# Products on column tiles, an FFN in 11 chunks and other orders of sums in a latent-attention kernel with an FFN gate

## The chip, the cores and the metric

The kernel runs on one core of one Trainium2 chip. The time is device microseconds of one execution; runs are compared by their median. Engines: TensorE (PE in the profile; PEld are its weight loads), VectorE (DVE), ScalarE (ACT), GpSimd (POOL), and SyncE (SP), which only issues transfers here.

## The reference

The input x has 8 sequences of 256 tokens with 512 features, all in fp32. What is computed, cut to what matters:

```python
xn = layernorm(x)                                  # over the 512 features
c_q, c_kv = xn @ Wq_down, xn @ Wkv_down            # 512 -> 64 each
q_c = (c_q @ Wq_up)    # 128 heads of 4            k_c, v_c = c_kv @ Wk_up, c_kv @ Wv_up
q_r = xn @ Wq_rope     # 128 heads of 64           k_r = xn @ Wk_rope   # 64, shared by the heads
scores = (q_c . k_c + q_r . k_r) / sqrt(68)        # per sequence and head, 256 x 256
s = softmax(scores) @ v_c  ->  @ Wo                # 512 -> 512
lin(x, wq, A, B) = x @ tile(wq, 4).T + 0.5 * x @ A.T @ B.T     # FFN, hidden 1376, rank 2
g = silu(lin2(silu(lin1(xn)) * lin3(xn)))
out = x + s * g
```

The FFN's weights repeat four times along their input. So x @ tile(wq, 4).T is the sum of the four quarters of x, 128 features wide, times wq.

## The kernel before, in words

All queues are filled in the order of the program text; no scheduler moves anything. Each engine runs its instructions in that order, and all transfers stand in one queue on SP. PSUM is a pool of eight banks of 128 x 512 (`bank`).

**First phase (`first_phase`, L286).** It runs over four blocks of 512 tokens. `norm` (L337) normalizes four tiles of x on DVE, `turn` (L364) transposes them on TensorE (xpt, L370) and adds the quarters (xsum). `narrow` (L392) and `down` (L402) make the products over xn (pm, pp, L387) and keep them in DRAM; `down` also calls `sum_x` (L141), which writes three quarters of xn to DRAM as they are and makes four differences on POOL (L154) for the later products. Then come six units u of two pairs: `low` (L410) writes the rank-2 products of four row-tiled matmuls into four banks (px and py, L420), `main` (L425) adds the 128-wide products onto them (L434, L435), ACT takes silu of px (L437) and DVE multiplies with py (L438) into hT. The hidden 1376 is four quarters of 344, each cut in chunks of 128, 128 and 88; hence 12 chunks for each of the two products. After units 2, 4 and at the end of the block `low_out` (L440) makes the rank-2 product mid2 on column tiles of 32 (its bank is pm, L449) and sums hT over the four quarters on POOL (L460 to L462, the result is h). `gate_out` (L472) then makes four products pf over three chunks each (L477), ACT takes silu into gs (two buffers), and gs goes to DRAM (L482). In the last block the steps of `between` (L554) put the first work of attention among the units: load and sum weights (`sum_w`, L126), `prepare` (qk, L240), `values` (vps, column tiles of 32, L267) and four `Project`s.

**Project (L177).** The query product with Wq_rope is made with a scheme of seven 256-column products in place of eight. Each product is two matmuls of 128 x 128 weights (`product`, L165; the matmul is L168, its banks are named q), so a Project has 14. ACT copies four banks (L208), POOL and DVE combine them (L213 to L226).

**Attention.** 64 steps n (sequence and group of 16 heads), each in two halves. A half has 48 score matmuls, four side by side on 32 rows (L618), eight maxima on DVE (L631), 16 exponentials on ACT (L637), eight transposes on DVE (L647), and one Project for a step two ahead, until all 128 are made. The first half also has `weigh` (av, L664, four side by side on 32 columns, for the step before) and, for some n, `prepare` and `values`. `normalize` (L692) divides by the sums. `put` (L723) multiplies with Wo (po, L727), `give` (L735) multiplies by the gate on DVE, adds x on POOL and stores; `finish` is both. Six of eight sequences are finished within the loop, at the end of second halves. The last two are written out at the end of the text:

```python
    weigh(last, 0)
    gather(last, early)
    for b in (B - 2, B - 1):
        for i in range(2):
            put(b, i, range(KT - 1))
    weigh(last, 1)
    gather(last, late)
```

then the two normalizations, the last chunk of every po and the four `give`s.

Of the kernel before, what the change touches and what calls it, by code (L numbers as in the profile page):

```python
# [15 lines left out]
P = 128  # L16
# [8 lines left out]
NTB = NT // TB  # L25
F = 1376
FQ = F // 4
CH = [(0, 128), (128, 128), (256, 88)]
EPS = 1e-5
QSCALE = float((HD + R) ** -0.5)  # L30

# [2 lines left out]
def mla_ffn_gate_kernel(  # L34
# [122 lines left out]
    def load_xs(p):  # L157

        if p < B // 2:
            xsums[p] = {}  # L160
            for i in (0, 4, 5, 3, 1, 6, 2):
                xsums[p][i] = xsp.tile([P, 2, S], F32, tag=f"x{i}", name=f"x{i}_{p}")
                nc.sync.dma_start(out=xsums[p][i], in_=xs_d[p][:, i])

    def product(bank_, w, x, first):  # L165

        for c in range(2):
            nc.tensor.matmul(  # L168
                bank_,
                w[:, c],  # L170
                x[:, c],
                start=first and c == 0,
                stop=c == 1,
                skip_group_check=True,
            )

    class Project:  # L177

# [57 lines left out]
    def prepare(b, g):  # L236


        qk = bank(f"qk_{b}_{g}")
        nc.tensor.matmul(qk[:, :S], wupq_sb[:, g, :], acts[b][:, 0, :], start=True, stop=True)  # L240
        nc.tensor.matmul(qk[:, S:], wupk_sb[:, g, :], acts[b][:, 0, :], start=True, stop=True)  # L241
        qc = qcp.tile([P, S], F32, tag="qc", name=f"qc_{b}_{g}", bufs=3)
        nc.scalar.copy(qc, qk[:, :S])  # L243
        kc = qcp.tile([P, S], F32, tag="kc", name=f"kc_{b}_{g}", bufs=3)
        nc.scalar.mul(kc, qk[:, S:], QSCALE)
        qks[b, g] = qc, kc
# [39 lines left out]
    def first_phase(between):  # L286
# [3 lines left out]

        ck_sb = fw.tile([P, KT, P], F32, name="ck_sb")
        cks_sb = fw.tile([P, 1], F32, name="cks_sb")
        w1_sb = fw.tile([P, F], F32, name="w1_sb")
        w3_sb = fw.tile([P, F], F32, name="w3_sb")
        b13_sb = fw.tile([98, F], F32, name="b13_sb")
        w2_sb = fw.tile([P, 3, D], F32, name="w2_sb")
        a2_sb = fw.tile([P, 4, 3, 32], F32, name="a2_sb")
        f1 = pool("f1", 1, st)
# [3 lines left out]
        def load_x(tb):  # L302
            xts[tb] = []
            for n in range(4):
                t = f1.tile([P, D], F32, tag="xt", name=f"xt_{tb}_{n}", bufs=6)
                nc.sync.dma_start(out=t, in_=x[ds(tb * TB + n * P, P), :])
                xts[tb].append(t)

        load_x(0)
        with tc.tile_pool(name="ckr", bufs=1) as ckr:  # L310
            kr_raw = ckr.tile([P, KT, R], F32, name="kr_raw")
# [14 lines left out]
        nc.sync.dma_start(out=wdn_sb, in_=w_down.rearrange("(c p) m -> p c m", p=P))  # L326
        for n in range(2):
            for k in range(2):
                nc.sync.dma_start(
                    out=b13_sb[64 * n + 32 * k : 64 * n + 32 * k + 2, :],  # L330
                    in_=b13[32 * k : 32 * k + 2, :],
                )
        nc.sync.dma_start(out=w1_sb, in_=w1t)
        nc.sync.dma_start(out=w3_sb, in_=w3t)
        load_x(1)

        def norm(tb):  # L337
# [46 lines left out]
        def over_xn(tb, name, weights):  # L384
            ps = bank(f"{name}_{tb}")
            for c in range(KT):
                nc.tensor.matmul(  # L387
                    ps, weights[:, c, :], xnT[tb][:, c, :], start=(c == 0), stop=(c == KT - 1)
                )
            return ps  # L390

        def narrow(tb):  # L392
# [9 lines left out]
        def down(tb):  # L402
            c = f1.tile([P, TB], F32, tag="tmp", name=f"c_{tb}")
            nc.scalar.copy(c, over_xn(tb, "pp", wdn_sb))
            nc.sync.dma_start(out=cs_d[tb], in_=c)
            sum_x(tb, xnT[tb])

        sets, hTs, h4s, mid2ps = {}, {}, {}, {}

        def low(tb, u):  # L410

            n, qp = divmod(u, 2)
            off, rows = CH[n]
            sets[tb, u] = []
            for i in range(2):
                cols = ds((2 * qp + i) * FQ + off, rows)
                for k in range(2):
                    ps = bank(f"p{'xy'[k]}_{tb}_{u}_{i}")
                    r = slice(64 * i + 32 * k, 64 * i + 32 * k + 2)
                    nc.tensor.matmul(  # L420
                        ps[:rows, :], b13_sb[r, cols], mids[tb][r, :], start=True, stop=False
                    )
                    sets[tb, u].append(ps)

        def main(tb, u):  # L425
            n, qp = divmod(u, 2)
            off, rows = CH[n]
            if qp == 0:
                hTs[tb, n] = f2.tile([P, 4, TB], F32, tag="hT", name=f"hT_{tb}_{n}")
            for i in range(2):  # L430
                q = 2 * qp + i
                cols = ds(q * FQ + off, rows)
                px, py = sets[tb, u][2 * i : 2 * i + 2]
                nc.tensor.matmul(px[:rows, :], w1_sb[:, cols], xsum[tb], start=False, stop=True)  # L434
                nc.tensor.matmul(py[:rows, :], w3_sb[:, cols], xsum[tb], start=False, stop=True)  # L435
                gate = f2.tile([P, TB], F32, tag="gate", name=f"gate_{tb}_{u}_{i}")
                nc.scalar.activation(gate[:rows, :], px[:rows, :], AF.Silu)  # L437
                nc.vector.tensor_mul(hTs[tb, n][:rows, q, :], gate[:rows, :], py[:rows, :])  # L438

        def low_out(tb, n):  # L440


            off, rows = CH[n]
            h = hTs.pop((tb, n))
            if n == 0:
                mid2ps[tb] = bank(f"pm2_{tb}")
                h4s[tb] = f1.tile([P, 3, TB], F32, tag="h4", name=f"h4_{tb}")
            for q in range(4):
                nc.tensor.matmul(  # L449
                    mid2ps[tb][32 * q : 32 * q + 32, :],  # L450
                    a2_sb[:rows, q, n, :],
                    h[:rows, q, :],
                    start=(n == 0),
                    stop=(n == 2),
                )
            if n == 2:
                nc.gpsimd.memset(h4s[tb][64:96, n, :], 0.0)
            h4 = h4s[tb][:rows, n, :]
            h4b = f1.tile([P, TB], F32, tag="h4b", name=f"h4b_{tb}_{n}")
            nc.gpsimd.tensor_add(h4, h[:rows, 0, :], h[:rows, 1, :])  # L460
            nc.gpsimd.tensor_add(h4b[:rows], h[:rows, 2, :], h[:rows, 3, :])
            nc.gpsimd.tensor_add(h4, h4, h4b[:rows])  # L462
            if n == 2:
                m2 = mid2ps.pop(tb)
                to = h4s[tb][96:128, n, :]
                nc.scalar.mul(to, m2[0:32], 0.5)
                for q in range(1, 4):
                    nc.vector.scalar_tensor_tensor(
                        to, m2[32 * q : 32 * q + 32], 0.5, to, ALU.mult, ALU.add
                    )  # L470

        def gate_out(tb):  # L472
            for n in range(4):
                tt = ds(n * P, P)
                pf = bank(f"pf_{tb}_{n}")
                for k in range(3):
                    nc.tensor.matmul(  # L477
                        pf, h4s[tb][:, k, tt], w2_sb[:, k, :], start=(k == 0), stop=(k == 2)
                    )
                gs = f2.tile([P, D], F32, tag="gs", name=f"gs_{tb}_{n}")  # L480
                nc.scalar.activation(gs, pf, AF.Silu)
                nc.sync.dma_start(out=gates_d[4 * tb + n], in_=gs)  # L482

        norm(0)
        turn(0)
        narrow(0)
# [4 lines left out]
        for tb in range(NTB):  # L491
            more = tb + 1 < NTB
            for u in range(6):
                low(tb, u)
                main(tb, u)
                if u in (2, 4):
                    low_out(tb, u // 2 - 1)
                if u == 1 and more:
                    norm(tb + 1)
                if u == 1 and tb + 2 < NTB:  # L500
                    load_x(tb + 2)
                if tb == NTB - 2 and u == 1:
                    between(1)
                if not more:
                    between(u + 2)
            if more:
# [4 lines left out]
            else:  # L511
                low_out(tb, 2)
            gate_out(tb)
        between(8)
        st.close()

# [206 lines left out]
    def put(b, n, chunks):  # L723
        if (b, n) not in pos:
            pos[b, n] = bank(f"po_{b}_{n}")
        for c in chunks:
            nc.tensor.matmul(  # L727
                pos[b, n],
                outT[b][:, c, ds(n * P, P)],
                wo_sb[:, c, :],  # L730
                start=(c == 0),
                stop=(c == KT - 1),
            )

    def give(b, n):  # L735
        g, xr = gxs.pop((b, n))
        nc.vector.tensor_mul(g, pos[b, n], g)  # L737
        nc.gpsimd.tensor_add(g, g, xr)
        nc.sync.dma_start(out=out[ds(b * S + n * P, P), :], in_=g)

    def finish(b, n):
# [10 lines left out]
    for n, (b, sg) in enumerate(blocks):  # L752
        for half in range(2):
# [18 lines left out]
            else:  # L772
                for r in range(4):
                    exponentials(n, two, r)
            for r in range(4):
                transpose(n, one, r)
            for r in range(2):
# [15 lines left out]
            if half == 0:  # L793
# [13 lines left out]
                        values(b + 1)  # L807
                if sg == 2 and b >= 2:
                    load_act(b + 2)
            elif n in outs:  # L810
                finish(*outs[n])


    early, late = ds(0, P), ds(P, P)
    weigh(last, 0)
    gather(last, early)
    for b in (B - 2, B - 1):
        for i in range(2):
            put(b, i, range(KT - 1))
    weigh(last, 1)  # L820
    gather(last, late)
    load_out(B - 2, 0)
# [2 lines left out]
    load_out(B - 1, 1, True)  # L825
    normalize(last - 1)
    normalize(last, early)
    put(B - 2, 0, [KT - 1])
    put(B - 2, 1, [KT - 1])
    put(B - 1, 0, [KT - 1])  # L830
    give(B - 2, 0)
    give(B - 2, 1)
    normalize(last, late)
    put(B - 1, 1, [KT - 1])
    give(B - 1, 0)
    give(B - 1, 1)


# [64 lines left out]
```

## Time and profile before

| | |
|---|---|
| three runs | 2059.2, 2064.73, 2066.32 us; median 2064.73 |
| the profiled execution | 2066.51 us, its span 2064.7 us |
| first phase, until the first scores start | 258.0 us |
| last scores of the loop end | 2039.7 us |
| maxima (L631) and transposes (L647) on DVE | 635.7 and 635.1 us busy |
| exponentials on ACT (L637) | 817.1 us busy |
| transfers | 183.15 MB, mean 89 GB/s |

How to read the profile: the page gives the busy time of each engine and the chain of work that ended last, followed back from the last instruction to what released each step. The same chain can be listed in order of time, merged where one line follows itself: start, length, engine, tile, line, count. The view by windows gives for a stretch its length, the busy time of an engine with the number of instructions, the granted TensorE clock, the share and the rate of DMA. An x before a number is a count. A matmul of fp32 operands is written once and stands in the trace as two records. Idle time of an engine is put down to what ended it.

### The profile page before, as it was taken

Reading aid. Unit: us, or ns where it says so; the run is one execution under the profiler, and the core shown is the slowest. Engines: PE = TensorE matmul, PEld = TensorE weight load, DVE = VectorE, ACT = ScalarE, POOL = GpSimd, SP = SyncE. Lnnn points to the kernel's source line nnn. Section 1 sums busy time; section 2 is a strip of 40 time slices with the busy share of each in tenths; the row PEclk is TensorE's granted clock in tenths of the full one; section 3 lists DMA queues with packets and bytes.
Section 4 is the critical chain, followed back from the end, with each engine's and each line's share of the span. In section 5 each row is a group of like instructions: output and inputs, shape, how many; then the busy total and the mean of one; then the engine's idle time right before and its main releaser. Section 6 shows DMA issues by size and latency. Waiting matters only on the chain.

```text
span 2064.7 us, 61156 instructions
## 1 busy us (share of the span) xinstructions
PE 2037.4 (99%) x25536; PEld 1665.3 (81%) x25536; DVE 1526.4 (74%) x2605; ACT 1084.0 (52%) x2991; POOL 718.4 (35%) x1039
## 2 busy tenths in 40 slices
PE   7999999999999999999999999999999999999998
PEld 3334588888888888888888888888888888888885
DVE  5332177878888777878788777878786867888788
ACT  2222265555655645465556554555555545555654
POOL 5334535544453232323332233223323223232232
PEclk9999999999999999999999999999999999999999
DMA  4233232222223132312223123222222222222212
GB/s 164 84 110 120 77 114 83 83 72 75 83 83 129 63 109 83 112 64 84 83 83 116 66 90 115 81 83 83 69 95 101 85 91 78 83 83 76 70 53 68
DMA packets 115447, 183.15 MB, mean 89 GB/s; under 512 B 8730, under 2 KB 81050, under 8 KB 115172
## 3 DMA queue, kind: packets, MB, share of 16 engines
q1 hardware_dynamic: 115172, 179.23, 25.2%
q8 instruction: 203, 3.33, 0.6%
q14 instruction: 72, 0.59, 0.1%
HBM read 145.12 MB, written 34.08 MB: 87 GB/s over the span
## 4 chain that ended last, share of the span: by engine, by line
PE 97%; DVE 1%; POOL 1%; DMA 0%; issue 0%; ACT 0%; POOLq 0%; SPq 0%; ACTq 0%; DVEq 0%
PE q L168 39%; PE sc L618 33%; PE av L664 11%; PE po L727 2%; PE px L434 2%; PE pf L477 2%; PE py L435 2%; PE px L420 1%; PE pm L387 1%; PE vps L267 1%; PE qk L240 1%; PE qk L241 1%; PE pp L387 1%; PE pm L449 1%; PE xpt L370 0%; DVE pt L647 0%
## 5 line engine op out<-in xcount | busy, mean ns | idle before, releaser
L637 ACT ACTIVATE pr<-sc,nmx 128x256 f32<-128x256 f32 x2048 | 817.1, 503 | 487.5 <-DVE nmx L631 486.0
L631 DVE TENSOR_REDUCE nmx<-sc 128x2 f32<-128x512 f32 x1024 | 635.7, 683 | 343.4 <-PE sc L618 314.2
L647 DVE STREAM_TRANSPOSE pt<-pr 128x512 f32<-128x512 f32 x1024 | 635.1, 678 | 0.0
L618 PE MATMUL sc<-act,qr 32*128 32x256 f32 x8192 | 492.1, 374 | 0.7 <-issue 0.6
L168 PE MATMUL q<-x,ws 128*128 128x256 f32 x2048 | 483.9, 379 | 0.0
L213 POOL TENSOR_TENSOR e<-e,e 128x256 f32<-128x256 f32 x128 | 93.1, 727 | 1083.6 <-ACT e L208 558.7
L618 PEld LDWEIGHTS sc<-act,qr 32*128 32x128 f32 x8192 | 423.5, 185 | 23.2 <-issue 1.4
L168 PEld LDWEIGHTS q<-x,ws 128*128 128x128 f32 x2048 | 389.0, 190 | 51.4 <-issue 0.2
L168 PE MATMUL q<-x,w 128*128 128x256 f32 x1536 | 387.4, 388 | 1.0 <-ACT pr L637 1.0
L168 PEld LDWEIGHTS q<-x,w 128*128 128x128 f32 x1536 | 291.5, 196 | 70.6 <-ACT pr L637 40.9
L618 PE MATMUL sc<-kc,qcm 32*128 32x256 f32 x4096 | 284.0, 387 | 2.1 <-DVE g L737 1.5
L618 PEld LDWEIGHTS sc<-kc,qcm 32*128 32x128 f32 x4096 | 199.8, 184 | 51.5 <-issue 24.2
L664 PEld LDWEIGHTS av<-pt,vpad 128*32 128x32 f32 x8192 | 219.6, 110 | 22.0 <-POOL e L214 8.0
L664 PE MATMUL av<-pt,vpad 128*32 128x128 f32 x8192 | 237.1, 273 | 0.0
L208 ACT COPY e<-q 128x256 f32<-128x256 f32 x512 | 203.6, 399 | 16.6 <-PE q L168 16.4
L684 ACT ACTIVATE acc<-av,sides_sb 128x256 f32<-128x256 f32 (+1 forms) x130 | 54.2, 468 | 235.7 <-PE av L664 235.7
L252 POOL TENSOR_TENSOR qcm<-qc,mask_sb 128x1024 f32<-128x1024 f32 x64 | 122.3, 1911 | 6.5 <-ACT qc L243 6.5
L438 DVE TENSOR_TENSOR hT<-gate,py 128x512 f32<-128x512 f32 (+1 forms) x48 | 32.5, 685 | 109.1 <-PE py L435 108.9
L215 POOL TENSOR_TENSOR qr<-e,e 128x256 f32<-128x256 f32 x128 | 93.6, 731 | 10.0
L214 POOL TENSOR_TENSOR e<-e,e 128x256 f32<-128x256 f32 x128 | 93.3, 729 | 10.0
L282 POOL COPY vpad<-vall 32x128 f32<-32x128 f32 x256 | 76.4, 298 | 18.9 <-ACT vall L274 5.8
L225 DVE TENSOR_TENSOR qr<-e,q 128x256 f32<-128x256 f32 x128 | 54.0, 422 | 29.1 <-PE q L168 20.6
(92 smaller groups left out, 1124.9 us busy)
## 6 DMA issues: line engine op xcount, KB each, us to landing
w<-in_w_rope_dram SPq DMA_DIRECT2D x128, 512.0 KB
ws<-sums_d SPq DMA_DIRECT2D x96, 512.0 KB
sums_d<-ws SPq DMA_DIRECT2D x32, 512.0 KB
x<-xs_d SPq DMA_DIRECT2D x28, 256.0 KB
xt<-in_x_dram SPq DMA_DIRECT2D x16, 256.0 KB
xs_d<-xt SPq DMA_DIRECT2D x16, 256.0 KB
gate_d<-gs SPq DMA_DIRECT2D x16, 256.0 KB
g<-gate_d SPq DMA_DIRECT2D x16, 256.0 KB
```

Source lines behind the costliest of these rows:

```text
L168: nc.tensor.matmul(bank_, w[:, c], x[:, c], start=first and c == 0, stop=c == 1, skip_group_check=True,)
L208: nc.scalar.copy(self.e[i], self.banks[i])
L213: nc.gpsimd.tensor_add(m6, m6, m1)
L214: nc.gpsimd.tensor_add(m7, m7, m6)
L215: nc.gpsimd.tensor_add(self.out(1, 1), self.split(m7), self.split(m5))
L252: nc.gpsimd.tensor_mul(qcm, qks[b, sg // 2][0].rearrange("p (q i) -> p q i", i=32).unsqueeze(2).to_broadcast([P, 8, 4, 32]), mask_sb[:, ds ...
L282: nc.gpsimd.tensor_copy(vpad[rows, :, :, 8 * t + 4 * (sg % 2) :][..., :4], valls[b][rows, :, sg])
L618: nc.tensor.matmul(sc[r][:, h, :], lhs.rearrange("p t i -> p (t i)"), rhs, start=(part == 0 and h == 0), stop=(part == 2), skip_group_chec ...
L631: nc.vector.tensor_reduce(nmx[:, r, :], scs[n, f][r], AX.X, ALU.max, negate=True)
L637: nc.scalar.activation(p[:, h, :], scs[n, f][r][:, h, :], AF.Exp, bias=nmxs[n, f][:, r, h : h + 1])
L647: nc.vector.transpose(pts[n, f // 2, r].rearrange("p k q i -> p q k i")[:, ds(2 * (f % 2), 2)], prs.pop((n, f, r)).rearrange("p h (k j) -> ...
L664: nc.tensor.matmul(av[32 * r : 32 * r + 32, ds(half * P, P)], vpad[:, k, r, :], pt[r][:, k].rearrange("p q i -> p (q i)"), start=(k == 0), ...
```

## The change

- A helper `on_columns` replaces one matmul of 128-wide weights by four with 32 columns of the weights each, which write to 32 partitions of the same bank each. It is used for all products that had 128-wide weights in `product`, `prepare`, `over_xn`, `main`, `gate_out` and `put`. Scores, the low products and the transposes stay as they are.
- The FFN's chunks of 88 in four quarters become three chunks of 128: the first 96 rows of chunk 8 + m hold the 88 of quarter m and zeros, the last 32 rows hold a third of the fourth quarter. The weights are loaded in pieces to match, four transfers in place of one for each of six pieces, and POOL sets zeros first. For these chunks the product on DVE is two instructions. The last unit has one chunk.
- The sums of hT on POOL are a function of their own, `fold`, called ahead of `low_out`, and for the last chunk right after unit 5, ahead of the `between` step there.
- `sum_x` leaves `down` and comes after unit 2 of the block (in the last block after unit 0).
- `gate_out` takes four banks at once and makes the first two chunks of all four products before the third chunk of any.
- 16 transposes of the identity come before the first `norm`.
- An exponential of one column comes on ACT behind the last `gate_out`.
- In step 62 `finish` comes ahead of the transposes of its half. At the end, the first three chunks of po are made ahead of the last `weigh` for one sequence, not two; the rest follows it in another order, and the last addition is on DVE.

```diff
+    def on_columns(to, w, x, start, stop):
+        for t in range(4):
+            tile_ = slice(32 * t, 32 * t + 32)
+            nc.tensor.matmul(to[tile_], w[:, tile_], x, start=start, stop=stop, skip_group_check=True)
+
     def product(bank_, w, x, first):
         for c in range(2):
-            nc.tensor.matmul(bank_, w[:, c], x[:, c], start=first and c == 0, stop=c == 1, ...)
+            on_columns(bank_, w[:, c], x[:, c], first and c == 0, c == 1)
...
+        def load_chunks(to, of):
+            of = of.rearrange("p (q f) -> p q f", q=4)
+            nc.sync.dma_start(
+                out=to[:, 0:8].rearrange("p (q n) m -> p q (n m)", q=4), in_=of[:, :, 0:256]
+            )
+            nc.sync.dma_start(out=to[:, 8:11, 0:88], in_=of[:, 0:3, 256:344])
+            nc.sync.dma_start(
+                out=to[:, 8:10, 96:128],
+                in_=of[:, 3, 256:320].rearrange("p (m i) -> p m i", m=2),
+            )
+            nc.sync.dma_start(out=to[:, 10, 96:120], in_=of[:, 3, 320:344])
+
+        for t in (w1_sb, w3_sb, b13_sb):
+            nc.gpsimd.memset(t[:, 8:11, 88:96], 0.0)
+            nc.gpsimd.memset(t[:, 10, 120:128], 0.0)
...
             nc.sync.dma_start(out=cs_d[tb], in_=c)
-            sum_x(tb, xnT[tb])
...
+        def pair(u):
+            return [2 * (i % 4) + i // 4 if i < 8 else i for i in range(2 * u, min(2 * u + 2, NCH))]
...
-                nc.tensor.matmul(px[:rows, :], w1_sb[:, cols], xsum[tb], start=False, stop=True)
-                nc.tensor.matmul(py[:rows, :], w3_sb[:, cols], xsum[tb], start=False, stop=True)
+                on_columns(px, w1_sb[:, c], xsum[tb], False, True)
+                on_columns(py, w3_sb[:, c], xsum[tb], False, True)
                 gate = f2.tile([P, TB], F32, tag="gate", name=f"gate_{tb}_{u}_{i}")
-                nc.scalar.activation(gate[:rows, :], px[:rows, :], AF.Silu)
-                nc.vector.tensor_mul(hTs[tb, n][:rows, q, :], gate[:rows, :], py[:rows, :])
+                nc.scalar.activation(gate, px, AF.Silu)
+                if c < 8:
+                    nc.vector.tensor_mul(h[:, c // 2, :], gate, py)
+                else:
+                    m = c - 8
+                    nc.vector.tensor_mul(h[0:96, m, :], gate[0:96], py[0:96])
+                    nc.vector.tensor_mul(
+                        h[32 * m : 32 * m + 32, 3, :], gate[96:128], py[96:128]
+                    )
...
         def gate_out(tb):
+            pfs = [bank(f"pf_{tb}_{n}") for n in range(4)]
+            for ks in ((0, 1), (2,)):
+                for n in range(4):
+                    for k in ks:
+                        on_columns(
+                            pfs[n], h4s[tb][:, k, ds(n * P, P)], w2_sb[:, k, :], k == 0, k == 2
+                        )
...
+        idle = bank("idle")
+        for n in range(16):
+            nc.tensor.transpose(idle[:, ds(n % 4 * P, P)], ident, ident)
         norm(0)
...
                 if u in (2, 4):
+                    fold(tb, u // 2 - 1)
                     low_out(tb, u // 2 - 1)
                 if u == 1 and more:
                     norm(tb + 1)
+                if u == (2 if more else 0):
+                    sum_x(tb, xnT[tb])
...
+                if u == 5:
+                    fold(tb, 2)
                 if not more:
                     between(u + 2)
...
             gate_out(tb)
+        nc.scalar.activation(cks_sb, cks_sb, AF.Exp)
         between(8)
...
-    def give(b, n):
+    def give(b, n, engine=nc.gpsimd):
         g, xr = gxs.pop((b, n))
         nc.vector.tensor_mul(g, pos[b, n], g)
-        nc.gpsimd.tensor_add(g, g, xr)
+        engine.tensor_add(g, g, xr)
...
+            if n == last - 1 and half:
+                finish(*outs[n])
             for r in range(4):
                 transpose(n, one, r)
...
     weigh(last, 0)
     gather(last, early)
-    for b in (B - 2, B - 1):
-        for i in range(2):
-            put(b, i, range(KT - 1))
+    for i in range(2):
+        put(B - 2, i, range(KT - 1))
     weigh(last, 1)
...
     normalize(last, early)
-    put(B - 2, 0, [KT - 1])
-    put(B - 2, 1, [KT - 1])
+    normalize(last, late)
+    put(B - 1, 0, range(KT - 1))
+    for i in range(2):
+        put(B - 2, i, [KT - 1])
     put(B - 1, 0, [KT - 1])
-    give(B - 2, 0)
-    give(B - 2, 1)
-    normalize(last, late)
-    put(B - 1, 1, [KT - 1])
-    give(B - 1, 0)
-    give(B - 1, 1)
+    put(B - 1, 1, range(KT))
+    for b in (B - 2, B - 1):
+        for i in range(2):
+            give(b, i, nc.vector if (b, i) == (B - 1, 1) else nc.gpsimd)
```

## The prediction

> **What bounds the kernel now.** I read the page first (busy shares, then the chain that ended last), next the chain in order of time in three stretches, and last the granted clock around the places where TensorE stood still. The page:
>
> ```profile
> PE 2037.4 (99%) x25536; PEld 1665.3 (81%) x25536; DVE 1526.4 (74%) x2605; ACT 1084.0 (52%) x2991; POOL 718.4 (35%) x1039
> ...
> PE q L168 39%; PE sc L618 33%; PE av L664 11%; PE po L727 2%; PE px L434 2%; PE pf L477 2%; PE py L435 2%; PE px L420 1%; PE pm L387 1%; PE vps L267 1%; PE qk L240 1%; PE qk L241 1%; PE pp L387 1%; PE pm L449 1%; PE xpt L370 0%; DVE pt L647 0%
> ```
>
> TensorE carries 97% of the chain, so every nanosecond it gives back counts until another engine is late. A product written once shows as two records here (28 for the 14 of a Project); I call one such record, or four side by side in tiles, a pass. The chain in order of time (start, length, what), from the attention loop:
>
> ```profile
> 474.39 5.39 PE sc L618 x96
> 479.78 6.25 PE q L168 x28
> 486.03 3.63 PE av L664 x128
> 489.66 5.39 PE sc L618 x96
> ...
> 706.53 3.63 PE av L664 x128
> 710.16 1.75 PE vps L267 x64
> ```
>
> and from the first phase:
>
> ```profile
> 210.25 1.06 PE px L434 x2
> 211.31 0.86 PE py L435 x2
> ...
> 213.88 6.04 PE q L168 x28
> ```
>
> The same 28 passes take 6.25 after the scores and 6.04 after py, which is also an untiled product. 6.04 / 28 = 215.7 ns is therefore the pass itself, and 0.21 the price of entering untiled products from row tiles. px says the same: 1.06 after the row-tiled low products against 0.86 in the middle, 0.20. vps runs on column tiles of 32 and follows av on such tiles: 1.75 / 16 = 109.2 ns a pass and no entry price. av after q is 3.63 - 32 x 0.1092 = 0.136. At 2039.70 av follows scores, not q, and 64 records take 1.89 = 1.75 + 0.14. So there are three prices: 0.21 into 128-wide weights from another layout, 0.136 into 32-wide ones, 0 within one layout. Scores pay 0.21 after q as after av (5.39 both times).
>
> **Column tiles, steady part.** q becomes 3584 passes of four instructions. Both ends: 32-wide passes of 128 columns take 109.2, twice that is 218.4, +2.7 ns a pass or +9.7 us; pm2 (32-wide, 512 columns, 0.99 for two) takes (0.99 - 0.136) / 2 = 427 ns against 429 for the untiled py, -1 ns at 256 columns or -3.6 us. I take 0: 256 columns lie between the two, and so does 0. A rule speaks against this change. The Trainium skill, "TensorEngine Tiling (Array Packing)", section Instruction Overhead, gives each matmul some 60 cycles; at the 2.4 GHz of "TensorE: Matmul & The Clock Gate" that is 25 ns. Added for three more instructions a pass, an estimate from these pages, it is 3584 x 75 ns = 269 us. The av row has 8192 records in 64 x 3.63 us, 28 ns each with their work in it, so the overhead lies under the neighbours' streaming; four in 215.7 ns are more thinly spread still. I follow the row.
>
> **Column tiles, entries.** Scores to q, 124 times (128 Projects, four of them in the first phase): 0.21 to 0.136, -9.1 (ends: 0, if the mode and not the width sets the price, and -9.1). q or qk to av, 61 times: 0.136 to 0, -8.3 (ends 0 and -8.3; av to vps is the same transition). In the first phase: low to px 24 x 0.065 = -1.6; px/py to pm2, to vps, and the last Project to pm2: 10 x 0.136 = -1.4; after pm2 the next product is in its layout: 3 x 0.20 + 2 x 0.21 + 0.20 = -1.2. The transposes stay untiled, so px/py to xpt newly pays 3 x 0.20, xpt to pm in block 0 0.14: +0.7. Together -20.9. What is late next: DVE waited for scores 126 times, 314.2 us in all, 2.5 each; a half loses under 0.25, so DVE stays ahead. If it did not, this part would stop there.
>
> **FFN in 11 chunks.** Each block's last unit keeps one chunk of two, so four of its eight px and py passes go, 4 x 0.429 = 1.72 us; the low products run side by side on row tiles and save nothing. Four blocks make 6.9, less 0.2 since 88-wide entries (1.02 for 1.06) become 128 wide: -6.7. DVE gets two more products of 0.68 a block; it idles 1 us between such products, and if that cover were gone it would be 1.4 a block.
>
> **fold and gate_out.** The last block ends like this:
>
> ```profile
> 242.32 0.74 POOL qr L215
> 243.11 0.53 POOL h L457
> ...
> 246.28 1.26 POOL h L462
> 247.53 0.04 issue
> 247.58 10.53 PE pf L477 x20
> 258.11 0.03 ACTq L481
> 258.14 0.04 issue
> 258.18 0.60 ACT gs L481
> 258.79 0.02 issue
> 258.81 3.39 DMA gate_d<-gs
> ```
>
> TensorE idles 2.18 for sums that stand behind the last Project's on POOL, and then runs slowly (20 passes in 10.53 instead of 8.6). The fold now goes first on POOL (some 4.3 us, its input ready about 4.5 before the Project ends), and 16 passes (6.9 us) cover the scaling of mid2 (about 3.2). pf shrinks from 14.7 to 10.3. But the four pf now finish 0.86 apart at the end, and gs has two buffers: gs 2 waits for the transfer of gs 0 (3.4), and behind it on ACT stand gs 3, the table load and the exponentials. Reckoned from the start of pf: gs 0 done at 8.5, gs 2 at 12.5, gs 3 at 13.3, landed at 16.8, first maxima and exponentials 17.5, q at 18.4. Before, 243.41 to 264.52 is 21.1. That is -2.7, although the table load (1.28) is off this path. TensorE then idles 2.7 instead of 1.03, and the clock view tells what such a gap did:
>
> ```profile
> 46.00:49.50 3.50, 1.70 (x6) 1.00 0.02 8
> 49.50:53.00 3.50, 3.50 (x6) 0.51 0.01 2
> 53.00:56.50 3.50, 3.50 (x21) 1.00 0.00 0
> 244.00:247.50 3.50, 1.40 (x4) 1.00 0.21 71
> 247.50:251.00 3.50, 3.42 (x4) 0.51 0.01 2
> ```
>
> (Fourth column: granted clock.) Gaps of 2.29 and 2.18 were each followed by some 3.4 us at half clock, a loss of 1.7. I charge 1.4 of it: -1.3 net (ends +1 and -4.4). In other blocks the late gs delays the first gate by 0.8, before its bank is needed.
>
> **Identity transposes.** The first 16 transposes took 3.65 against 1.91 later, pm 5.75 against 3.70: at most 3.8 to gain. The identities run from about 1.4 to 5.0, then nothing until x is normalized at 10.16. A gap of 5.1 is more than twice the gaps that cost the clock, so I take 0 (ends +1 and -3.8). "TensorE: Matmul & The Clock Gate", Part 4, says that transposes do not count as busy for the clock; by it the gain is 0 whatever the gap. Here 1.75 us of transposes at 60.5 left no slow stretch behind, so the gap is my reason, not the rule.
>
> **Other orders.** sum_x moves behind norm in blocks 1 and 2. Four POOL operations (1.27 each) then meet norm on DVE. In block 0 they meet today: four normalizations took 5.66 instead of 1.92 and the small steps 3.4 instead of 0.8, which made the 2.29 gap. Block 0 keeps the same POOL work in another order, so I leave its gap. In blocks 1 and 2 DVE would be some 2.8 late and low of unit 4 about 0.25 each: +0.5 (ends 0 and +8, with gap and slow clock twice). On SP the xs_d transfers go from before to after the gates; the last block's x sums then load some 5 later, landing 4 before use: 0, and a microsecond each if late. The chunked loads add 18 transfers on SP, about 0.5 each: 9.5 us more, so that SP is through at some 18.5; the next in the queue, kr_d, waits for mid until 21.25: 0, with w3 some 5 early. If that cover is gone, px waits: up to +3. The six memsets lie before a load that POOL awaits until 7.84.
>
> **Tail.** Behind the last scores DVE sets the time (transposes end at 2047.02), and then 24 po passes hold back the last av until 2052.09. Now 12 passes (5.2) end before the transposes, the other 20 (8.6) run after av, beside normalize. I get the last product about 2058.2, its multiply 0.69 and add 0.69 on DVE: 2059.8 against 2061.7, -1.9. Taken off: finish moved ahead of DVE's transposes makes DVE wait about 0.6 for po with eight transposes behind it, which the next av awaits (in the 2059.8), and a gap of 2.2 before the last av can halve the clock: +0.9. Net -1.0 (ends +1 and -3).
>
> **Sum.** -20.9 - 6.7 - 1.3 - 1.0 + 0.5 = -29.4. The profiled execution took 2066.51 (span 2064.7, 1.8 around it), and is 1.8 above the median 2064.73. 2066.5 - 29.4 = 2037.1; beside the median, 2035.3. I say 2036.
>
> **Rivals.** (1) Width does not matter for entering: the 9.1 and 1.6 stay, 2047. For it: row and column modes both differ from untiled, and only av, 32 wide, shows the lower price. (2) Neither entry gains, since q and av are different shapes of one layout: about 2056; av to vps speaks against it, though both have 128 columns. (3) The clock is kept through the start and block 0 loses its gap: 3.8 + 4 more, 2028. (4) Slower: four instructions a pass cost time in steady state, at L168. The break-even is 29.4 / 3584 = 8.2 ns a pass; at 230 ns it ends at 2087. For it: four reads of one x at once with strided weights, which no row shows; against it: vps and pm2. (5) POOL and DVE collide in blocks 1 and 2 at full price: 2044.
>
> Chances: mine 0.53, (1) 0.16, (2) 0.07, (3) 0.12, (4) 0.05, (5) 0.07. Range 2026 to 2050: it holds mine with the steady part's ends, (1), (3) and (5), and leaves out (2) and (4). Faster by over 0.3% (6.2 us, about what a measurement of this kernel can tell from no change) 0.92, within 0.04, slower 0.04.
>
> **What would show it.** q after scores 6.18, av after q 3.49, q after untouched layout 6.04: entries right; 6.25 means (1), 6.3 or more in all places means (4). pf in 10.3 and a first q about 18.4 after its start; pm at the start still near 5.7; no gap over 1 us in blocks 1 and 2; last add on DVE about 2.9 before the end. I am wrong if passes in the middle of q stretch, or if the half-clock stretches number more than four.

## The result, and the profile after

| | before | after |
|---|---|---|
| median of the runs | 2065.53 us (4 runs) | 2049.45 us (4 runs, 2047.66 to 2051.7) |
| profiled execution (span) | 2066.51 (2064.7) | 2051.7 (2049.9) |

The ratio is 0.9928, 95% interval 0.9904 to 0.9952: about half of the gain that was forecast. The page of the changed kernel, busy times and the start of the chain that ended last:

```profile
PE 2019.9 (99%) x38048; PEld 1416.2 (69%) x38048; DVE 1537.2 (75%) x2614; ACT 1080.7 (53%) x2988; POOL 720.1 (35%) x1044
...
PE 95%; DVE 3%; DMA 1%; issue 1%; ACT 0%; SPq 0%; DVEq 0%; ACTq 0%
```

Records on TensorE grow by half, its busy time falls by 17.5 us, and it still carries 95% of the chain. Transfers and issue now hold 1% each. The chain in order of time (start, length, what), in three places:

```profile
210.48 6.04 PE q L172 x112
...
472.73 5.39 PE sc L657 x96
478.12 6.18 PE q L172 x112
484.30 3.49 PE av L703 x128
...
707.11 1.51 PE vps L269 x50
708.62 0.57 issue
709.19 0.64 PE vps L269 x14
```

q behind scores, av behind q, and q behind a product of its own layout take 6.18, 3.49 and 6.04, to the hundredth what was forecast. vps, in one piece of 1.75 in four of its six stages before, now has a hole in all six. Next, the border of blocks 0 and 1, where the kernel before went from the transposes into pm without a hole of this size:

```profile
54.27 1.04 PE xpt L387 x8
55.33 0.37 SPq L308
...
56.72 3.66 DMA xs_d<-act
60.50 1.30 DVE act L392 x2
```

The chain leaves TensorE after half of the transposes and returns by way of SP, a transfer and DVE; pm follows at 61.94. The queue of SP there (start, length until the last was issued):

```profile
31.53 24.16 SPq L308 DMA_DIRECT2D xt<-in_x_dram x4
55.74 1.54 SPq L149 DMA_DIRECT2D xs_d<-act x3
```

`load_x` of block 2 (L308) waits at the head of the queue until the transposes of block 1 give up their xt buffers. The three transfers of `sum_x`, which read block 0's xnT (one buffer, act), stand behind it, and the copies of block 1's transposes into that same buffer wait for them (12.8 us on ACT and 9.5 on DVE in two waits each). It happens again at 113. By windows (length, PE, PEld, DVE, ACT and POOL busy, granted clock, DMA):

```profile
58.50:62.00 3.50, 0.06 (x4) 0.10 (x8) 1.40 (x3) 1.50 (x3) 0.11 (x2) 1.00 1.07 400
62.00:65.50 3.50, 3.50 (x20) 1.15 (x24) 2.27 (x4) 0.16 (x1) 1.71 (x1) 0.51 0.10 39
...
96.00:99.50 3.50, 3.05 (x20) 0.73 (x21) 3.36 (x5) 1.73 (x3) 2.87 (x3) 1.00 0.00 0
99.50:103.00 3.50, 3.50 (x20) 0.87 (x16) 3.38 (x7) 0.97 (x2) 0.68 (x1) 0.51 0.00 0
```

Besides the start, the first phase has four half-clock stretches (the others at 120.0 and 157.6). pm takes 5.34 behind each of the two long waits and 3.64 in block 3, so each wait costs another 1.70.

A table of stages for all runs, from the starts of the transposes and products in each trace. A block runs from its first transpose to that of the next, block 3 to the first q of the loop; "loop" ends with the last scores; "end" is the rest of the span. vps is the sum of its six stages in the loop. The runs were made on several chips, on which the kernel before had medians from 2061.76 to 2065.53, so kernels are compared by their ratios, or by stages.

| kernel | block 0 | 1 | 2 | 3 | first q | loop | end | vps | median | ratio to before (95%) |
|---|---|---|---|---|---|---|---|---|---|---|
| before | 50.2 | 50.9 | 50.9 | 102.3 | 264.5 | 1775.2 | 25.0 | 12.2 | 2065.53 | |
| after | 44.8 | 57.8 | 58.0 | 94.8 | 264.9 | 1761.7 | 23.4 | 17.0 | 2049.45 | 0.9928 (0.9904 to 0.9952) |
| e1_sums_down | 40.1 | 49.2 | 49.2 | 94.9 | 242.7 | 1762.1 | 23.3 | 18.2 | 2030.85 | 0.9845 (0.9830 to 0.9859) |
| e2_before_sums_late | 48.9 | 59.3 | 60.4 | 99.9 | 278.5 | 1773.6 | 25.0 | 11.5 | 2080.98 | 1.0086 (1.0073 to 1.0100) |
| e3_before_columns | 45.4 | 50.6 | 50.6 | 98.4 | 254.9 | 1762.8 | 24.5 | 16.3 | 2045.14 | 0.9912 (0.9899 to 0.9925) |
| e4_q_whole | 43.5 | 57.9 | 58.0 | 96.0 | 264.8 | 1774.7 | 23.3 | 11.8 | 2064.58 | 1.0010 (1.0001 to 1.0020) |
| e5_sums_first | 45.8 | 49.2 | 49.2 | 95.1 | 248.9 | 1762.7 | 23.4 | 18.2 | 2034.89 | 0.9864 (0.9847 to 0.9881) |
| e6_values_later | 45.1 | 57.9 | 57.9 | 95.0 | 265.2 | 1757.5 | 23.6 | 10.5 | 2048.04 | 0.9930 (0.9917 to 0.9944) |
| e7_best1 | 47.7 | 49.2 | 49.2 | 95.2 | 251.7 | 1755.1 | 23.3 | 10.5 | 2031.85 | 0.9848 (0.9832 to 0.9863) |
| e8_old_fold | 47.6 | 49.2 | 49.2 | 96.9 | 253.8 | 1763.6 | 23.4 | 19.9 | 2040.87 | 0.9893 (0.9877 to 0.9909) |
| e9_load_later | 40.0 | 51.5 | 51.4 | 95.3 | 247.4 | 1762.9 | 23.3 | 17.6 | 2037.56 | 0.9873 (0.9859 to 0.9886) |
| e10_no_idle | 46.3 | 49.2 | 49.2 | 94.8 | 249.6 | 1758.2 | 23.4 | 12.8 | 2033.04 | 0.9849 (0.9836 to 0.9862) |
| e11_best | 42.6 | 49.2 | 49.2 | 95.2 | 245.6 | 1756.3 | 23.5 | 10.5 | 2027.36 | 0.9822 (0.9808 to 0.9835) |
| e12_best_no_idle | 44.2 | 49.2 | 49.2 | 94.8 | 247.3 | 1754.3 | 23.5 | 10.5 | 2025.79 | 0.9818 (0.9804 to 0.9831) |

Before to after, the span loses 13.5 in the loop and 1.6 at the end, and the first phase gains nothing (+0.4) where 11.0 were forecast.

### The profile page after: what moved, and what is told of

Read it like the earlier page. It is cut to its first block, busy times and chain, and to the rows that moved or that the text cites. A ratio compares the mean times of both kernels' runs of the same rounds, so it can differ in the third digit from the quotient of the medians.

```text
span 2049.9 us, 86481 instructions
## 1 busy us (share of the span) xinstructions
PE 2019.9 (99%) x38048; PEld 1416.2 (69%) x38048; DVE 1537.2 (75%) x2614; ACT 1080.7 (53%) x2988; POOL 720.1 (35%) x1044
## 3 DMA queue, kind: packets, MB, share of 16 engines
HBM read 145.12 MB, written 34.08 MB: 87 GB/s over the span
## 4 chain that ended last, share of the span: by engine, by line
PE 95%; DVE 3%; DMA 1%; issue 1%; ACT 0%; SPq 0%; DVEq 0%; ACTq 0%
PE q L172 39%; PE sc L657 33%; PE av L703 11%; PE po L172 2%; PE pf L172 2%; PE px L172 2%; PE py L172 2%; PE qk L172 1%; PE pm L172 1%; PE px L436 1%; PE vps L269 1%; PE pp L172 1%; DVE pt L686 1%; DVE st L358 0%; DVE nmx L670 0%
## 5 line engine op out<-in xcount | busy, mean ns | idle before, releaser
L172 PE MATMUL q<-x,ws 128*32 128x256 f32 x8192 | 488.8, 379 | 0.0
L172 PEld LDWEIGHTS q<-x,ws 128*32 128x32 f32 x8192 | 264.9, 110 | 177.2 <-issue 0.5
L172 PE MATMUL q<-x,w 128*32 128x256 f32 x6144 | 381.4, 381 | 0.6 <-ACT pr L676 0.6
L172 PEld LDWEIGHTS q<-x,w 128*32 128x32 f32 x6144 | 186.2, 110 | 154.9 <-ACT pr L676 40.1
L703 PEld LDWEIGHTS av<-pt,vpad 128*32 128x32 f32 x8192 | 226.3, 110 | 14.5 <-issue 3.0
L210 ACT COPY e<-q 128x256 f32<-128x256 f32 x512 | 203.3, 398 | 15.2 <-PE q L172 14.8
L284 POOL COPY vpad<-vall 32x128 f32<-32x128 f32 x256 | 74.8, 292 | 16.3 <-ACT vall L276 5.6
L453 DVE TENSOR_TENSOR hT<-gate,py 128x512 f32<-128x512 f32 x32 | 21.5, 685 | 73.8 <-PE py L172 73.4
L227 DVE TENSOR_TENSOR qr<-e,q 128x256 f32<-128x256 f32 x128 | 53.9, 421 | 26.2 <-PE q L172 18.2
```

The lines of the kernel that those rows point to most:

```text
L172: nc.tensor.matmul(to[tile_], w[:, tile_], x, start=start, stop=stop, skip_group_check=True)
L210: nc.scalar.copy(self.e[i], self.banks[i])
L284: nc.gpsimd.tensor_copy(vpad[rows, :, :, 8 * t + 4 * (sg % 2) :][..., :4], valls[b][rows, :, sg])
L703: nc.tensor.matmul(av[32 * r : 32 * r + 32, ds(half * P, P)], vpad[:, k, r, :], pt[r][:, k].rearrange("p q i -> p (q i)"), start=(k == 0), ...
```

## The experiments

Theory A: the first phase's gain is there and is given back by the new place of `sum_x`, through the order on SP. Rival B: column tiles, chunked loads or the new product order cost the first phase. Theory C concerns the loop: vps runs out of instructions behind the longer stream. (The expectations below, put down before each run, call a unit a chunk set.)

**sum_x back in its old place.**

```diff
             nc.sync.dma_start(out=cs_d[tb], in_=c)
+            sum_x(tb, xnT[tb])
...
-                if u == (2 if more else 0):
-                    sum_x(tb, xnT[tb])
```

> The changed kernel with sum_x put back where it was (at the end of down). Theory A: the first phase loses its gain because, with sum_x in chunk set 2, the transfers that read the transposed block (xs_d<-act) are queued on SP behind load_x of the block after next, and the next block's copies out of PSUM wait for them twice (4.8 and 4.9 us of idle TensorE, and some 1.7 us each of half clock behind it). Then both idles go, the first q of the loop starts near 252 us instead of 264.9, and the time is 11 to 15 us below the changed kernel's 2049.5: about 2036. Rival B: the first phase loses by the column tiles, the chunked loads or the new order of the last product; then the place of sum_x is worth within 3 us, and the first q stays near 265 us.

2030.85, and both holes are gone. The border of blocks 1 and 2:

```profile
98.62 1.90 PE xpt L387 x16
...
101.63 3.64 PE pm L172 x32
```

All 16 transposes in one piece, and narrow's pm at full clock; between them lie low_out's pm and 0.12 us. Rival B falls. The gain, 18.6 us by the medians and 17 by the ratios, is more than A had reckoned: blocks 1 and 2 give 17.4, not 13, and this execution's block 0 was a short one (below).

**The same move alone, in the kernel before.** The edit of `sum_x` reversed: out of `down`, into unit 2, as in the change. `load_x` is called in unit 1 and so stands ahead of it on SP.

> The kernel before with one thing changed: sum_x is called in chunk set 2 (in the last block, set 0), as in the changed kernel. Theory A: the two waits of the next block's copies for xs_d<-act appear here too, 4.5 to 7 us each with the half clock after them, and the time rises by 8 to 14 us (about 2076), the first q of the loop moving from 264.5 to 273 to 278 us. Rival B: within 3 us of the kernel before.

2080.98: +17.4 us, above the range. Its waits show the new wait, which the kernel before does not have:

```profile
ACT act L373 <- DMA xs_d<-act: 13.8, 2, 7.2
```

(us in all, times, the longest; VectorE waits another 11.8 us for the same transfers.) Blocks 1 and 2 grow by 8.4 and 9.5. One part of the change, moved alone, costs as much as the whole change gained.

**Column tiles alone, in the kernel before.** `on_columns` in `product`, `prepare`, `over_xn`, `main` (88 rows as 32, 32 and 24), `gate_out` and `put`; nothing else of the change.

> The kernel before with one thing changed: every product but the scores, the transposes and the narrow products of two rows is made in column tiles of 32 (chunks as before, so 88 rows make tiles of 32, 32 and 24). Theory A: the loop loses as much as in the changed kernel, 12 to 13 us (8 at the entries into q, 8.5 into av, less 4 to 5 given back as issue idle in vps), and the first phase gains 3 to 5 us: 2049 to 2051, the first q of the loop near 261 us. Rival B: the tiles cost the first phase more than they gain there: the first q at 264.5 us or later, 2053 or more. The prediction's sum for this part alone was -20.9 us, 2044.

2045.14: -18.5 us against a forecast of -20.9, and 4 us below Theory A's range. The tiles alone are no slower than the whole change (0.9912 and 0.9928, with overlapping intervals). The loop gives 12.4. Blocks 1 and 2 give 0.3 each, blocks 0 and 3 4.8 and 3.9: these two are where the kernel before had its half-clock stretches, and this trace has none behind the start; its first pm took 3.64 and not 5.75.

**q whole in the changed kernel.** `product` makes one matmul of 128 columns again.

> The changed kernel with the q products alone as one product of 128 columns again (28 records in a q stage instead of 112). The entries come back: 124 x 0.066 us at q and 62 x 0.137 us at av, +16.7 us. Theory C: the idle inside the vps stages (6 stages of 2.8 us instead of 1.75) comes from the four times longer instruction stream of the q stage ahead of it; then vps falls back to 1.75 to 2.0 us a stage, and the sum is +12 us: about 2061. If the stream of q has nothing to do with it, vps stays at 2.8 us and the sum is +17 us: 2066.

2064.58, 15.1 above the changed kernel by the medians and 17 by the ratios, so the time alone does not choose between the two numbers. The traces do: the loop is 13.0 longer, and vps falls to 11.8, four of its six stages to 1.75. That speaks for Theory C.

The traces hold the cause itself. The page counts the transfers of instructions (queue, kind: packets, MB, share), before and after:

```profile
q8 instruction: 203, 3.33, 0.6%
```

```profile
q8 instruction: 301, 4.93, 1.0%
```

With q whole there are 217. TensorE's records (PE and PEld) are 51072 before and 76096 after, some 252 a packet both times, so this queue brings TensorE's instructions. The trace keeps the time of each packet. In the changed kernel one landed at 707.90, 1.29 us before the hole of vps shown above ended at 709.19. All 44 holes in vps stages, over all 14 traces, end 1.2 to 1.6 us behind such a landing, and so do the two longest holes in the scores of the changed kernel's loop (0.48 and 0.21 us). TensorE stood waiting for its own instructions; Theory C is shown.

**Sums one set earlier.**

```diff
-                if u == (2 if more else 0):
+                if u == (1 if more else 0):
                     sum_x(tb, xnT[tb])
```

> The changed kernel with sum_x one chunk set earlier, so that on SP its seven transfers stand ahead of load_x of the block after next instead of behind it; on POOL its four subtractions stay ahead of fold. Theory A (the queue order on SP is the cause): the reads xs_d<-act have landed long before the next block's copies, both idles of 4.8 and 4.9 us and their half clock go, the first q of the loop comes between 243 and 250 us (242.7 with sum_x in down), time 2031 to 2038. Rival (the place on POOL is the cause: subtractions in the middle of a block, beside VectorE's products and ahead of fold): most of the loss stays, first q at 256 us or later, 2042 or more.

2034.89; blocks 1 and 2 take 49.2 as with the old place. The expectation overlooked that this moves the subtractions ahead of the first fold on POOL as well, so the run does not part queue order from the place on POOL. The next run does.

**load_x behind sum_x.**

```diff
-                if u == 1 and tb + 2 < NTB:
-                    load_x(tb + 2)
                 ...
                     sum_x(tb, xnT[tb])
+                if u == 2 and tb + 2 < NTB:
+                    load_x(tb + 2)
```

> The changed kernel with load_x of the block after next called in chunk set 2 behind sum_x, not in set 1 ahead of it: only the order of the two on SP changes, while sum_x keeps its place on POOL (behind the first fold). This parts what the run with sum_x one set earlier moved together. Theory A: the two idles of 4.8 and 4.9 us ahead of pm and the half clock behind each go, 6.4 us a block; what the subtractions on POOL cost beside VectorE in sets 2 to 4 stays, 2 to 2.5 us in each of the blocks 1 and 2: blocks of 51 to 52 us instead of 57.8 and 58.0 (49.2 with sum_x in down), first q near 252 us, time 2036 to 2040. If the place on POOL is what holds the copies, the idles stay and the time is 2049.

2037.56, blocks of 51.5 and 51.4. SP's queue in block 1:

```profile
71.72 1.54 SPq L149 DMA_DIRECT2D xs_d<-act x3
...
87.93 14.22 SPq L308 DMA_DIRECT2D xt<-in_x_dram x4
```

`load_x` still waits 14 us for its buffers, but nobody stands behind it who is needed: the reads went out some 29 us before the copies. So the order on SP is worth 6.3 and 6.6 us a block, and 2.3 and 2.2 belong to the subtractions' place on POOL. What that is shows in `norm`, where VectorE meets the subtractions on POOL. First the changed kernel:

```profile
93.80 1.28 POOL L157 TENSOR_TENSOR xt<-act 128x512 f32<-128x512 f32 x1
94.35 0.75 DVE L362 TENSOR_SCALAR ve<-mv 128x4 f32<-128x4 f32 x1
...
96.39 1.26 POOL L157 TENSOR_TENSOR xt<-act 128x512 f32<-128x512 f32 x1
96.48 1.19 DVE L369 TENSOR_TENSOR e<-e,ve 128x4 f32<-128x4 f32 x1
```

then with `sum_x` in `down`:

```profile
83.15 0.17 DVE L362 TENSOR_SCALAR ve<-mv 128x4 f32<-128x4 f32 x1
...
84.00 0.16 DVE L369 TENSOR_TENSOR e<-e,ve 128x4 f32<-128x4 f32 x1
```

Operations on four elements a partition take 0.75 and 1.19 us and end within 0.02 us of the subtraction on POOL. The Trainium skill, "SBUF — State Buffer", section "SBUF: two separate sides", says that VectorE and GpSimd share one port pair under an exclusive lock, and the loser waits for the whole instruction of the other; on VectorE's side it names operations with two SBUF inputs, as L369 has, and those in a two-port mode. The ends of these rows agree; in which mode L362 ran, no row shows. The chain goes through L362, not L369:

```profile
94.35 0.76 DVE ve L362
95.36 1.28 ACT L451
96.65 0.61 ACT gate L451
97.30 1.12 PE py L436 x2
```

ve is 0.58 late, so ScalarE comes late to the silu that frees a bank, and the last products of `low` start after 0.45 us of idle. The half clock of 1.7 follows: 2.2 together. The run with `load_x` behind `sum_x` has the same chain, with ve at 82.98.

**values() in the second half.** It is called behind q of the second half, which av does not follow.

```diff
-                if (sg == 7 and b % 2) or (sg == 0 and b and b % 2 == 0):
-                    if b + 1 < B:
-                        values(b + 1)
...
+            if half and ((sg == 7 and b % 2) or (sg == 0 and b and b % 2 == 0)) and b + 1 < B:
+                values(b + 1)
```

> The changed kernel with values() called in the second half of its pass, so that in the six places of the loop the vps stage follows a q stage and not an av stage; nothing else moves. Theory C: a stage of 64 records at 27 ns runs TensorE out of instructions only when it follows the 128 records at 27 ns of av, behind a q stage of 112 records; alone behind q it finds them. Then vps falls from 2.8 to 1.75 to 2.0 us a stage, 5 to 6.5 us in all: about 2044. If the density of the instructions has nothing to do with it, vps stays at 2.7 us or more and the time at 2049.

All six vps stages take 1.75. The chain:

```profile
712.02 6.18 PE q L172 x112
718.21 1.75 PE vps L269 x64
```

6.5 us less in vps make 4.1 in the loop; stages of scores that run longer than 5.39 take 2.3 more in this trace. The median, 2048.04, does not tell this run from the changed kernel, and the 2044 of the expectation was missed.

**Both.** `sum_x` in `down`, and values() as above.

> sum_x in down again (2030.9 alone) and values() in the second half of its pass: if the two causes add, 2024 to 2026; if the stages of the loop only move their idle elsewhere, 2030.

2031.85, a miss by its median. The loop is 7.0 shorter than with `sum_x` in `down` alone, so the causes add there; block 0 is 7.6 longer. Block 0 takes two courses from trace to trace. VectorE's four passes over x in it, here (three of the four in one row) and with `sum_x` in `down` alone:

```profile
40.77 4.42 DVE L376 TENSOR_SCALAR xt<-xt,mv,rstd 128x512 f32<-128x512 f32 x3
```

```profile
36.03 2.88 DVE L376 TENSOR_SCALAR xt<-xt,mv,rstd 128x512 f32<-128x512 f32 x4
```

Here POOL's first subtraction began at 39.45, before the passes; there at 37.26, when three of the four were done. Of the 7.6 us, 2.9 are these passes (5.82 in all), 2.3 the first pm (5.91, not 3.64), and some 1.7 a half-clock stretch at 50.2. That fits the spread of executions by some 5 us (one at 2026.59, three from 2031.81 to 2032.51 for this kernel). The kernel before takes the long passes in its profile, and so does the changed kernel (5.70 for the four). What decides at the start whether POOL or VectorE comes first was not settled.

**Old fold.** `sum_x` in `down`; fold behind low_out's matmuls, the products of `gate_out` one after another, no early Exp.

> sum_x in down again (2030.9 alone), and fold, the order of the last FFN product and the early Exp as in the kernel before: what these three are worth without the stalls. The prediction's term says 1.3 us (2032.2). Theory A says 3 to 6 us (2034 to 2037): the last product's wait for POOL, 2.2 us, and the half clock that followed it come back in the last block, and the loop's first Exp starts later; first q near 246 to 248 us instead of 242.7.

2040.87, 4 us above the upper end of Theory A's range. Blocks 1 and 2 do not change; block 3 is 2.0 longer. Its chain there:

```profile
238.37 1.26 POOL h L474
...
239.67 8.79 PE pf L172 x80
```

The wait for POOL ahead of the last pf is back, but not the half clock. Block 0 of this trace took its long course (above) and is 7.5 longer than with `sum_x` in `down`, so the stage and not the median tells what these three are worth: 2.0.

**No identities**, twice: with `sum_x` in `down`, and in the fastest version.

> sum_x in down again (2030.9), without the 16 transposes of the identity while x loads. The prediction says they are worth 0: 2029 to 2033. If they warm TensorE for the first products, the first narrow product starts later or runs at the slower pace and the time is 2 to 4 us longer. The start of block 0 differs by some 5 us between executions of one kernel, so the page of this run decides by the start of pm and not the median alone.

> The fastest version so far (2027.4: sum_x in down, values() in the second half, norm of block 1 one set earlier) without the 16 identity transposes. Its block 0 no longer takes two courses, so the identities can be told from the start's scatter here. The prediction's 0: 2025.5 to 2029. If they keep TensorE warm, the first 16 transposes or the first pm take 1.7 us or more longer and the time is 2029 or more; if they hold up the start themselves, below 2025.5.

2033.04 (0.9849) beside 0.9845 with them, 2025.79 (0.9818) beside 0.9822: no difference that these runs can tell. The first pm took 5.4 with identities in the changed kernel and without them in the last run, and 3.6 in others of either kind, so the identities do not decide it. The clock does: in all 14 traces the first pm takes 3.6 to 3.7 where the clock is recorded as full before it starts, and 5.4 to 5.9 where that comes later, at 17.6 us or after. A side finding: in the first of the two, three vps stages fell to 1.75 (12.8 in all) though only records at the very start of the program were left out. Without them the stream is cut into packets at other places.

**The fastest version.**

```diff
-                if u == 1 and more:
+                if u == (1 if tb else 0) and more:
                     norm(tb + 1)
```

on top of "both".

> sum_x in down, values() in the second half of its pass, and norm of block 1 one chunk set earlier in block 0, so that VectorE's four passes over x are done before the subtractions of sum_x start on POOL. In three of four profiles those four passes took 5.8 us instead of 2.9 beside POOL and held up the products behind them. If so, block 0 takes 40 to 42 us (47.7 in the profile of the run without this step) and the time is 2025 to 2028 in nearly all executions; if not, 2032.

2027.36 (executions from 2025.77 to 2028.21). The four passes, at 34.08, take 2.63 in all, and block 0 takes 42.6, a little over the 40 to 42 expected: low_out's pm, which waits for VectorE behind the passes, now takes 4.1 in place of 0.86. With the identities left out as well, it is 2025.79, a ratio 0.011 below the changed kernel's, 23 us.

## Why the prediction was only half right

The forecast was -29.4; the changed kernel's span fell by 14.8, its median by 16.1. 2049.45 lies just inside the range of 2026 to 2050, and that is luck: the range reached so far up for rivals (1) and (5), and most of the loss came from neither. Of the signs that were named, "no gap over 1 us in blocks 1 and 2" failed, with 4.9 and 4.8; the half-clock stretches came to four, the most that was allowed.

**The step that failed** is "sum_x moves behind norm in blocks 1 and 2 ... +0.5 (ends 0 and +8, with gap and slow clock twice)". It followed the four subtractions to POOL and, on SP, only to the last block's loads; it did not ask which queue entry the three direct transfers stand behind now, and who waits for the buffer that they read. Measured: 17.4 us in blocks 1 and 2, of which 12.9 is the order on SP and 4.5 POOL. The collision itself was forecast, at 0.5, and rival (5) priced it at 8: its 4.5 lies between. The other 12.9 was on no list. Without this step the sum was -29.9, and the run with `sum_x` in `down` gives -32.8 in the medians. That they are so close is in part luck: its trace has the short course of block 0, 10.1 less than before and far more than was forecast there, and vps gives back 6.0 that the sum had at 0.

**Column tiles, steady part (0) and entries (-20.9).** Right in kind and nearly in size. The steady pass did not move, although a rule spoke for 269 us more: 112 instructions of q take 6.04. In the loop 123 q stages save 0.067 and 61 to 62 av stages 0.137, 16.7 of the 17.4 forecast. But vps gave 4.8 back, which the sum had at 0 because it checked only the layout; four instructions for one also mean more to load, and that was on no list either. In the first phase 3.5 were forecast; 0.3 shows in each of two blocks, and what blocks 0 and 3 gained can't be parted from their clock.

**11 chunks (-6.7).** e3_before_columns to e8_old_fold, which adds the chunks: 1.4 in each of blocks 1 and 2 and 1.5 in block 3, about 5.7 for four blocks if block 0 is like them. The missing 0.3 a block was not followed up.

**fold and gate_out (-1.3).** 2.0 in block 3, inside the ends. The reckoned end of that chain was too late: pf to the first q took 16.3, not 18.4.

```profile
248.57 8.63 PE pf L172 x80
...
257.85 2.04 DMA gate_d<-gs
...
260.97 3.01 DMA sums_d<-ws
```

In the changed kernel's chain the gate's transfer took 2.04 and not the 3.4 of before; TensorE idled 0.6 us ahead of the first q and not 2.7, and the half clock that was charged at 1.4 did not come. The first exponential waited for a transfer of `sum_w` and not for its table.

**Identities (0)** held, and for the reason given. The windows with `sum_x` in `down`, where the 16 identities end at 5.04:

```profile
5.30:8.70 3.40, 0.00 (x0) 0.00 (x0) 2.85 (x12) 0.20 (x1) 1.26 (x8) 1.00 0.66 147
8.70:12.10 3.40, 2.87 (x14) 2.88 (x15) 2.53 (x5) 0.60 (x2) 1.36 (x4) 0.50 0.04 6
```

The clock is full behind them, with TensorE idle, and half again when the transposes of x come. Four traces show this (from 4.3 to 5.3 us on, for 3.4 us), so transposes did raise the clock there, against the rule that the forecast set aside.

**Tail (-1.0):** the end shrank by 1.6, and by 0.5 with column tiles alone, so 1.1 is the new order. The last add ends 3.0 before the end; 2.9 was forecast.

**Chunked loads (0)** held: no wait of px or py for w1 or w3.

**The clock.** The forecast charged a half clock only behind gaps of about 2 us. The row of windows at 96.00, in the result above, shows one behind a stretch with 0.45 us of idle. The Trainium skill, "TensorE: Matmul & The Clock Gate", section "Why this matters for your kernels", advises against idle gaps over about 3 us; here much less was enough, and the measurement decides. The four stretches start at 62.00, 99.54, 120.02 and 157.57 and last 3.41 each; their distances are 11, 6 and 11 times 3.41. So in this trace the clock changes on a fixed grid, and where on the grid an idle falls may matter. What the clock counts in such a stretch (it holds the low products with two rows) stays open.

## What to carry to other kernels

When a step is moved, list its transfers too, and for each ask two things: what stands ahead of it in its queue and until when that waits, and who waits to overwrite what it reads. A prefetch that waits for a free buffer belongs behind every transfer whose completion frees a buffer. Splitting matmuls to keep one layout cost nothing in the stage itself here, but look at the dense stages of short instructions behind it: they may run out of instructions.

## What was not expected of the hardware

- vps, 64 records of 27 ns each, ran in 1.75 us behind q and in 2.7 to 3.0 behind q and av in the changed kernel (1.75 to 4.0 in the other runs with 112 records in q); with 28 records in q it was 1.75 to 2.7. Every hole in it ended 1.2 to 1.6 us after a packet of TensorE's instructions had landed. Which packets come too late depends on where a stage lies in the stream: leaving out records at the start of the program moved the holes.
- VectorE's work on 128 x 4 elements took 0.16 us alone and up to 1.20 beside POOL; block 0's four passes took 2.63 to 2.88 or 5.7 to 5.8.
